# Cross-attention and LoRA-MoE kernel: product 7 taken jointly for two pairs, with the steps around it resequenced

## The chip, the core and the metric

The kernel runs on one core of one Trainium2 chip. The metric is device time in microseconds (us) for one execution. Engines: PE does matrix multiplications, DVE elementwise work, ACT activations and copies, POOL (GpSimd) elementwise work between SBUF tiles, and SP issues the DMAs.

## The reference, cut to what is computed

```python
# x (8,1024,1024), ctx (8,64,1024), mask (8,64), weight (1024,1024)
# lora_A (8,16,1024), lora_B (8,1024,16), router_w (8,1024); float32
h = layernorm(x)
scores = einsum('bsd,bmd->bsm', h, ctx) / 32
scores = where(mask, scores, -1e30)
x = x + einsum('bsm,bmd->bsd', softmax(scores), ctx)     # 0 where no mask is set
h = layernorm(x)
base   = einsum('btd,od->bto', h, weight)
logits = einsum('btd,ed->bte', h, router_w)
w_dense = top-2 of softmax(logits), renormalised, 0 elsewhere
Ax = einsum('nd,erd->ner', h, lora_A)
x = x + base + 2.0 * einsum('ner,ne,eor->no', Ax, w_dense, lora_B)
```

## The kernel before

The 8192 rows of x are 64 tiles of 128 rows. Two tiles are a *pair* u (32 pairs), held in SBUF as `xts[u][0]` and `xts[u][1]`; all work is float32. The function `first()` handles pairs 0 and 1 and prepares sums of the weights. After that `quad(u)`, u = 2, 4, ... 30, handles two pairs u and v = u+1 for the big product and, in the same stretch, prepares later pairs: n = u+2 and m = u+3 get their attention readout and second normalisation, and f = u+4 gets its scores and softmax. There are 15 such quads.

**The big product.** h times weight for a pair is a 2 by 2 block product taken in the Strassen-Winograd form: seven products instead of eight. `block_sums` forms on POOL the four sums of blocks of h that this needs (s1 to s4, each 128x512, four instructions), `weight_sums` formed the sums of weight blocks (t1 to t4) once. A product of 512 columns is a *block* of four matmuls (`block`, each recorded as two in the profile). `product(u, i)` runs product i = 1, 6 or 7 of one pair, all three into one PSUM bank `ch`, the running chain; after each, `product_add` adds the bank into one quarter of the pair's rows of x: 1 to (row tile 0, column half 0), 6 to (0, 1), 7 to (1, 0). `product(u, 8)` is the low-rank (LoRA) term for (1, 1), added to the same bank and then into x.

Products 5, 3, 2 and 4 are taken for the two pairs at once by `joint(i, u, hooks)`: here the pair of pairs is itself split 2 by 2, so that again seven blocks stand in place of eight, each of two matmuls of 256 columns. Its sums of activations come from `joint_sums` (POOL), its sums of weights from `quarter_sums` (DVE, four instructions on 128x512 a weight). A joint product writes two banks, `jl` (lower) and `ju` (upper), each holding two results of 256 columns. Blocks run in the order p4, chain, p2, p5, chain, p5, chain; between them DVE must read a result into x before the next block may write on top of it (`part`, `to_x`, the group at L716). Product 5 goes into both row tiles, so each of its reads is two DVE instructions. `hooks[k]` are steps recorded after the k-th block.

**Around it.** For each pair: `load_xs`/`load_xt` bring x twice, blocked (for turning) and plain; `att_turn` turns the blocked copy on DVE; `att_scores` (PE, 32 matmuls, L367), `att_sc` (one transpose on PE), `att_exp`, `att_divide`, `att_turn_p` (one transpose on PE), `att_readout` (PE, four matmuls, L420) and `att_add` (DVE, four adds) are the attention. `x_stats` is three ACT steps over the rows (`x_sums`, `x_squares`, `x_root`); `f_sums`, `f_squares`, `f_std`, `f_rows` do the second normalisation, of which `f_rows` begins with two small DVE instructions, writes h on ACT and sends it through DRAM (`norm_send`, `norm_fetch`) so that it comes back blocked; `rt_turn` turns it (four DVE instructions for a pair). `rt_low_rank_tile` (PE, L513) gives LoRA and router products of one row tile, the second one ends with a copy on ACT; `rt_top` is the routing on DVE (some 17 small instructions, with one exponential on ACT between them); `rt_turn_low_rank` (PE, two transposes, L553) needs its result. `mask_bias`, `send_mem`, `turn_mem`, `void_mem` prepare the context of a new batch; that is so in every second quad (u = 4, 8, ... 24).

**Order.** The whole schedule is manual: each engine runs its instructions in the order in which the code records them. A step that waits therefore holds up all that is recorded behind it on its engine. SP issues all DMAs in one such queue. Tiles with one tag share `bufs` buffers of a pool, and a new tile waits for the last reader of the buffer it gets; `ring` (6 buffers of 128x1024) holds xs, turned x, h, and h fetched back.

Of the kernel before, what the change touches and what calls it, by code (L numbers as in the profile page):

```python
# [17 lines left out]
P = 128  # L18
# [6 lines left out]
def kernel(  # L25
# [38 lines left out]
    ring = ctx.enter_context(tc.tile_pool(name="ring", bufs=6))  # L64
# [59 lines left out]
    def load_w(kh: int, oh: int):  # L124
# [10 lines left out]
    mask_u8 = const.tile([P, B, M], U8, name="mask_u8")  # L135
    nc.sync.dma_start(
        out=mask_u8.rearrange("p b m -> p (b m)"),
        in_=mask.rearrange("b m -> (b m)").partition_broadcast(P),
    )
# [24 lines left out]
    def mask_bias(b: int):  # L164

        biases[b] = memp.tile([P, M], F32, tag="bias", name=f"bias_{b}")
        nc.vector.tensor_copy(biases[b], mask_u8[:, b, :])
        valids[b] = memp.tile([P, 1], F32, tag="valid", name=f"valid_{b}")
        nc.vector.tensor_reduce(valids[b], biases[b], AX.X, ALU.max)
        nc.vector.tensor_scalar(biases[b], biases[b], NEG, -NEG, ALU.mult, ALU.add)  # L170
# [17 lines left out]
    def x_sums(u: int):  # L188

        sm = small.tile([P, 2, 1], F32, tag="sm", name=f"sm_{u}")  # L190
        nm = small.tile([P, 2, 1], F32, tag="nm", name=f"nm_{u}")
        for r in range(2):
            nc.scalar.activation(  # L193
                nowhere, xts[u][r], AF.Identity, accum_out=sm[:, r, :]
            )
        nc.scalar.mul(nm, sm, -1.0 / D)
        stds[u] = nm

    def x_squares(u: int):
        ss = small.tile([P, 2, 1], F32, tag="ss", name=f"ss_{u}")  # L200
        for r in range(2):
            nc.scalar.activation(  # L202
                nowhere, xts[u][r], AF.Square, bias=stds[u][:, r, :],
                accum_out=ss[:, r, :],
            )
        stds[u] = ss

    def x_root(u: int):

        ss = stds[u]  # L210
        stds[u] = small.tile([P, 2, 1], F32, tag="std_att", name=f"std_att{u}")
        nc.scalar.activation(stds[u], ss, AF.Sqrt, bias=eps_sb[:, 1:2])
# [13 lines left out]
    def x_std(u: int):  # L226
        mv = xmv.pop(u)
        stds[u] = small.tile([P, 2, 1], F32, tag="std_att", name=f"std_att{u}")
        nc.scalar.activation(
            stds[u], mv[:, :, 1:2], AF.Sqrt, bias=eps_sb[:, 1:2], scale=float(D)  # L230
        )

    junk = const.tile([P, D], mybir.dt.bfloat16, name="junk")
# [4 lines left out]
    def f_sums(u: int):  # L238

        sm = small.tile([P, 2, 1], F32, tag="smf", name=f"smf_{u}")  # L240
        nm = small.tile([P, 2, 1], F32, tag="nmf", name=f"nmf_{u}")
        for r in range(2):
            nc.scalar.activation(
                nowhere, xts[u][r], AF.Identity, accum_out=sm[:, r, :]
            )
        nc.scalar.mul(nm, sm, -1.0 / D)
        fts[u] = nm

    def f_squares(u: int):
        nm = fts[u]  # L250
        ss = small.tile([P, 2, 1], F32, tag="ssf", name=f"ssf_{u}")
# [4 lines left out]
        fts[u] = nm, ss  # L256

    def f_std(u: int):
        nm, ss = fts[u]
        std = small.tile([P, 2, 1], F32, tag="stdf", name=f"stdf_{u}")  # L260
        nc.scalar.activation(std, ss, AF.Sqrt, bias=eps_sb[:, 0:1], scale=1.0 / D)
        fts[u] = nm, std

    def f_rows(u: int, fetch: bool = True):

        nm, std = fts.pop(u)
        rstd = small.tile([P, 2, 1], F32, tag="rstdf", name=f"rstdf_{u}")
        nc.vector.reciprocal(rstd, std)
        nmr = small.tile([P, 2, 1], F32, tag="nmrf", name=f"nmrf_{u}")
# [104 lines left out]
    def att_rstd(u: int):  # L374
        sts[u] = small.tile([P, 2, 1], F32, tag="rstd_att", name=f"rstd_att{u}")
        nc.vector.reciprocal(sts[u], stds.pop(u))
# [6 lines left out]
    def att_exp(u: int):  # L383
# [6 lines left out]
        mx = small.tile([P, 2], F32, tag="mx", name=f"mx_{u}")  # L390
        nc.vector.tensor_reduce(mx, s, AX.X, ALU.max, negate=True)
        den = small.tile([P, 2], F32, tag="den", name=f"den_{u}")
# [5 lines left out]
        ps[u] = s, den  # L398

    def att_divide(u: int):  # L400
        s, den = ps[u]
        rden = small.tile([P, 2], F32, tag="rden", name=f"rden_{u}")
# [30 lines left out]
    def norm_stats(u: int, r: int, at_once: bool = True):  # L433
        mv = small.tile([P, 2], F32, tag=f"mv_ffn{r}", name=f"mv_ffn{u}_{r}")
        row_stats(mv, xts[u][r], f"ffn{u}_{r}")
# [4 lines left out]
    def norm_std(u: int, r: int):  # L440
        mv = nst[u, r]
        std = small.tile([P, 1], F32, tag=f"std_ffn{r}", name=f"std_ffn{u}_{r}")
# [3 lines left out]
    def norm_rows(u: int, r: int, here: bool):  # L446

        mv, std = nst.pop((u, r))
        rstd = small.tile([P, 1], F32, tag=f"rstd_ffn{r}", name=f"rstd_ffn{u}_{r}")
# [68 lines left out]
    def rt_top(u: int):  # L518
# [6 lines left out]
        dl = small.tile([P, 2, 1], F32, tag="dl", name=f"dl_{u}")  # L525
        tt(dl, top[:, :, 1:2], top[:, :, 0:1], ALU.subtract)
        e2 = small.tile([P, 2, 1], F32, tag="e2", name=f"e2_{u}")
# [3 lines left out]
        idf = small.tile([P, 2, 2], F32, tag="idf", name=f"idf_{u}")  # L531
# [5 lines left out]
        w1 = small.tile([P, 2, 1], F32, tag="w1", name=f"w1_{u}")  # L537
        nc.vector.tensor_scalar(w1, e2, 1.0, None, ALU.add)
        nc.vector.reciprocal(w1, w1)
        w2 = small.tile([P, 2, 1], F32, tag="w2", name=f"w2_{u}")  # L540
# [32 lines left out]
    def rt_sums_steps(u: int):  # L573
# [3 lines left out]
            sums.tile([P, 2, HK, P], F32, tag=f"s{i}", name=f"s{i}_{u}").rearrange(  # L577
                "p h k i -> p (h k) i"
            )
            for i in (2, 3)  # L580
# [7 lines left out]
    def rt_sums(u: int):  # L588
        for do in rt_sums_steps(u):
            do()  # L590
# [17 lines left out]
    def quarter_sums(name: str, w):  # L608
# [4 lines left out]
        tt(q3, b22, b12, ALU.subtract)  # L613
        tt(q2, q3, b11, ALU.add)
        tt(b12, b12, b11, ALU.subtract)
        tt(q4, b21, q2, ALU.subtract)
# [39 lines left out]
    def product_add(u: int, i: int):  # L656
# [4 lines left out]
        else:  # L661
            add(u, chain, *{1: (0, 0), 6: (0, 1), 7: (1, 0), 8: (1, 1)}[i])


    L2 = {2: (0, 0), 3: (0, 1), 4: (1, 0), 5: (None, 1)}
# [14 lines left out]
    def joint_sums(i: int, u: int):  # L680

        tags = "s2", "s3", "q3", "q4"
        outs = [
            sums.tile([P, 2, HK, P], F32, tag=t, name=f"{t}_j{i}_{u}") for t in tags
# [9 lines left out]
    def joint(i: int, u: int, hooks, final: bool = False):  # L694
# [6 lines left out]
        r, c = L2[i]  # L701
        a, d = [
            {2: hbs[p][:, 0], 3: sms[p][:, 1], 4: hbs[p][:, 1], 5: sms[p][:, 0]}[i]
# [3 lines left out]
        name = {2: "w21", 3: "w22", 4: "t4", 5: "t1"}[i]  # L707
# [4 lines left out]
        def to_x(p, src, first: int, n: int):  # L712
            cols = slice(c * HB + first, c * HB + first + n)
            for row in (0, 1) if r is None else (r,):
                xc = xts[p][row][:, cols]
# [65 lines left out]
    def add_and_stats(u: int, r: int):  # L781
# [5 lines left out]
        mv = small.tile([P, 2], F32, tag=f"mv_ffn{r}", name=f"mv_ffn{u}_{r}")  # L787
        nc.vector.bn_aggr(mv, st)
# [5 lines left out]
    def first():  # L794
# [70 lines left out]
        load_mem(1)  # L865
        att_divide(1)
# [37 lines left out]
        rt_sums(1)  # L904
# [57 lines left out]
        quarter_sums("t1", t1)  # L962
        att_scores(4)
# [11 lines left out]
    def quad(u: int):  # L975
# [7 lines left out]
        product(u, 1, (lambda: att_sc(n)) if u == 2 else None, 1)  # L983
        pending.pop()()
        product_add(u, 1)
        rt_low_rank_tile(u, 0)
        rt_turn(v)
        product(u, 6)
        if more:
            x_stats(m)  # L990
        if u == 2:
            att_divide(n)
            att_turn_p(n)
        if more:
            att_turn(m)
        product_add(u, 6)
        if u == 2:
            quarter_sums("t4", t4)
        if new_mem:
            mask_bias(b)  # L1000
            send_mem(b)
        if far:
            load_xs(f)
            load_xt(f)
        rt_low_rank_tile(u, 1)
        product(u, 7)
        rt_top(u)
        product_add(u, 7)
# [5 lines left out]

        if more:
            product(v, 1, {0: lambda: att_sc(m), 2: lambda: product(u, 8)})
            att_rstd(m)
            att_exp(m)
            one, two = rt_sums_steps(v)
            one()  # L1020
            product_add(u, 8)
            product_add(v, 1)
            two()
            f_sums(n)
            att_divide(m)
            rt_low_rank_tile(v, 0)
            product(v, 6, lambda: att_turn_p(m), 1)
            f_squares(n)
        else:
            rt_sums(v)  # L1030
            product(v, 1, {0: lambda: rt_turn_low_rank(u), 2: lambda: product(u, 8)})
            product_add(u, 8)
            product_add(v, 1)
            rt_low_rank_tile(v, 0)
            product(v, 6)
        if far:
            att_turn(f)
        product_add(v, 6)
        rt_low_rank_tile(v, 1)
        product(v, 7)  # L1040
        if new_mem:
            turn_mem(b)
        rt_top(v)
        if more:
            f_std(n)
            f_rows(n)
        product_add(v, 7)
        one, two = joint_sums(5, u)
        one()
        if more:  # L1050
# [3 lines left out]
        if u == 2:  # L1054
            quarter_sums("w21", w21)
# [3 lines left out]
        two()  # L1059

# [4 lines left out]
        if more:  # L1065
            hooks = {2: [low_v]}
# [4 lines left out]
        if far:  # L1071
            x_sums(f)
            x_squares(f)
            x_root(f)
            hooks[3] = [lambda: att_sc(f)]
        end_5 = joint(5, u, hooks)

        hooks = {1: [end_5]}
# [3 lines left out]
        if far:  # L1082
            hooks[2] = [lambda: att_rstd(f), lambda: att_exp(f)]
            hooks[7] = [lambda: att_divide(f)]
        end_3 = joint(3, u, hooks)
        if m + 2 < NP:
            load_xs(m + 2)
            if (f + 2) % PPB == 0 and f + 2 < NP:
                load_mem((f + 2) // PPB)

        one, two = joint_sums(2, u)
        one()
        hooks = {1: [end_3], 2: [two]}
        if more:
            f_squares(m)
            f_std(m)
            hooks[1].append(lambda: f_rows(m, False))
# [5 lines left out]
        def rows_0():  # L1103
# [5 lines left out]
            if more:  # L1109
                norm_fetch(m)  # L1110
# [4 lines left out]
        if more:  # L1115
            hooks[5] = [lambda: rt_sums(n)]
# [59 lines left out]
```

## Time and profile before

| what | value |
|---|---|
| median of 3 runs | 1124.63 us (1124.46 to 1125.69) |
| the profiled execution's own time | 1124.92 us |
| its span from first to last instruction | 1123.1 us |
| POOL busy in the span | 312.4 us (28%) |
| clock granted to PE | full in every slice |
| PE waiting for another engine, all named waits together | under 6 us, most of it before 21 us |
| quads 4, 6, 8, ... (start to start of the first product) | 68.2 us each |
| quad 2 | 69.15 us |
| x rows (512 KB), issue to landing | 6.5 us median |
| stores of x (512 KB), issue to landing | 3.5 us median |

A row of a timeline below gives start, length, engine, line, operation, output and inputs, shape and count. Lengths of matmuls include the tail of a pipeline, so the pace of PE is read from start to start. L613 to L616 are the four instructions of `quarter_sums`, L564 to L569 those of `block_sums`, L622 the adds of `add`.

### The profile page before, as it was taken

Reading aid. Unit: us, or ns where it says so; the run is one execution under the profiler, and the core shown is the slowest. Engines: PE = TensorE matmul, PEld = TensorE weight load, DVE = VectorE, ACT = ScalarE, POOL = GpSimd, SP = SyncE. Lnnn points to the kernel's source line nnn. Section 1 sums busy time; section 2 is a strip of 40 time slices with the busy share of each in tenths; the row PEclk is TensorE's granted clock in tenths of the full one; section 3 lists DMA queues with packets and bytes.
Section 4 is the critical chain, followed back from the end, with each engine's and each line's share of the span. In section 5 each row is a group of like instructions: output and inputs, shape, how many; then the busy total and the mean of one; then the engine's idle time right before and its main releaser. Section 6 shows DMA issues by size and latency. Waiting matters only on the chain.

```text
span 1123.1 us, 15874 instructions
## 1 busy us (share of the span) xinstructions
PE 1113.6 (99%) x5490; PEld 774.0 (69%) x5490; DVE 743.1 (66%) x1855; ACT 553.4 (49%) x1047; POOL 312.4 (28%) x260
## 2 busy tenths in 40 slices
PE   8999999999999999999999999999999999999998
PEld 6555576675867768676685866758677686766867
DVE  6679887666676566866568656686666766665544
ACT  4575562735537354472635736356373544725010
POOL 0022233142223323233132331432233232331331
PEclk9999999999999999999999999999999999999999
DMA  9966255562654726538363464535545454452401
GB/s 222 232 197 197 75 169 186 171 203 93 180 175 139 243 86 181 166 114 262 99 193 122 151 225 131 188 125 161 184 132 188 158 161 151 113 188 75 151 1 75
DMA packets 104464, 175.75 MB, mean 156 GB/s; under 512 B 11904, under 2 KB 76544, under 8 KB 104384
## 3 DMA queue, kind: packets, MB, share of 16 engines
q1 hardware_dynamic: 104384, 174.73, 50.6%
q8 instruction: 44, 0.72, 0.3%
q14 instruction: 36, 0.29, 0.1%
HBM read 107.84 MB, written 66.85 MB: 156 GB/s over the span
## 4 chain that ended last, share of the span: by engine, by line
PE 98%; DVE 1%; DMA 0%; ACT 0%; issue 0%; SPq 0%; DVEq 0%; ACTq 0%
PE ch L633 28%; PE jl L633 18%; PE ju L633 14%; PE pa L513 11%; PE ro L420 5%; PE sct L367 5%; PE ju L625 3%; PE jl L625 3%; PE plain L633 3%; PE ch L625 2%; PE trw L553 1%; PE j L633 1%; DMA xt<-in_x_dram 0%; PE ptp L409 0%; PE tr_x L342 0%; DVE xt L622 0%
## 5 line engine op out<-in xcount | busy, mean ns | idle before, releaser
L716 DVE TENSOR_TENSOR xt<-jl,xt 128x256 f32<-128x256 f32 (+1 forms) x301 | 140.0, 486 | 164.5 <-PE jl L633 111.2
L633 PE MATMUL ch<-t,s 128*128 128x512 f32 x496 | 224.7, 592 | 0.0
L193 ACT ACTIVATE junk<-xt 128x1024 bf16<-128x1024 f32 x60 | 63.3, 1055 | 206.3 <-DMA xt<-in_x_dram 205.3
L633 PEld LDWEIGHTS ch<-t,s 128*128 128x128 f32 x496 | 88.5, 190 | 86.2 <-issue 86.1
L622 DVE TENSOR_TENSOR xt<-ch,xt 128x512 f32<-128x512 f32 x124 | 85.0, 685 | 58.8 <-PE ch L633 34.6
L716 DVE TENSOR_TENSOR xt<-ju,xt 128x256 f32<-128x256 f32 (+1 forms) x150 | 80.3, 552 | 63.5 <-PE ju L633 62.6
L633 PE MATMUL ch<-w,hA 128*128 128x512 f32 x248 | 115.9, 593 | 0.0
L564 POOL TENSOR_TENSOR s<-hA,hB 128x512 f32<-128x512 f32 x31 | 39.6, 1278 | 266.0 <-DVE hB L89 201.6
L274 ACT ACTIVATE h<-xt,nmrf,rstdf 128x1024 f32<-128x1024 f32 x60 | 71.2, 1233 | 39.9 <-DVE nmrf L270 39.9
L622 DVE TENSOR_TENSOR xt<-ro,xt 128x512 f32<-128x512 f32 x128 | 81.3, 683 | 11.9 <-PE ro L420 11.9
L513 PEld LDWEIGHTS pa<-art_sb,hA 128*128 128x128 f32 x512 | 68.5, 190 | 23.2 <-issue 18.6
L89 DVE STREAM_TRANSPOSE xT<-xs 128x1024 f32<-128x1024 f32 x60 | 71.3, 1218 | 5.8 <-DMA xs<-in_x_dram 5.8
L633 PEld LDWEIGHTS ch<-w,hA 128*128 128x128 f32 x248 | 44.7, 190 | 43.0 <-issue 42.1
L564 POOL TENSOR_TENSOR s_j<-s 128x512 f32<-128x512 f32 x15 | 19.1, 1275 | 187.4 <-PE ch L633 187.4
L202 ACT ACTIVATE junk<-xt,nm 128x1024 bf16<-128x1024 f32 x60 | 68.9, 1149 | 2.0
L513 PE MATMUL pa<-art_sb,hA 128*128 128x136 f32 x512 | 69.9, 279 | 0.0
L513 PE MATMUL pa<-art_sb,hB 128*128 128x136 f32 x512 | 69.7, 279 | 0.0
L253 ACT ACTIVATE junk<-xt,nmf 128x1024 bf16<-128x1024 f32 x60 | 68.8, 1146 | 1.1
L367 PEld LDWEIGHTS sct<-xT,memT_True 128*64 128x64 f32 x960 | 51.8, 137 | 22.7 <-issue 17.4
L564 POOL TENSOR_TENSOR s_j<-hB 128x512 f32<-128x512 f32 x15 | 19.0, 1268 | 172.5 <-PE ju L633 172.5
L513 PEld LDWEIGHTS pa<-art_sb,hB 128*128 128x128 f32 x512 | 64.1, 190 | 0.0
L420 PE MATMUL ro<-mem,pt 64*128 64x512 f32 x256 | 63.6, 615 | 0.4 <-ACT pt L411 0.4
(183 smaller groups left out, 2090.0 us busy)
## 6 DMA issues: line engine op xcount, KB each, us to landing
xt<-in_x_dram SPq DMA_DIRECT2D x64, 512.0 KB, 6.5
out_dram<-xt SPq DMA_DIRECT2D x62, 512.0 KB, 3.5
xs<-in_x_dram SPq DMA_DIRECT2D x240, 128.0 KB, 3.8
hd<-h SPq DMA_DIRECT2D x60, 512.0 KB, 2.7
hs<-hd SPq DMA_DIRECT2D x240, 128.0 KB, 3.4
mem<-in_ctx_dram SPq DMA_DIRECT2D x16, 256.0 KB, 5.5
w<-in_w_t_dram SPq DMA_DIRECT2D x16, 256.0 KB, 10.2
md<-memc_False SPq DMA_DIRECT2D x7, 256.0 KB, 2.9
```

Of the source, the lines that this page charges most:

```text
L89: nc.vector.transpose(dst.rearrange("p k (t i) -> p t k i", i=NB), src.rearrange("p t (k i) -> p t k i", i=NB),)
L202: nc.scalar.activation(nowhere, xts[u][r], AF.Square, bias=stds[u][:, r, :], accum_out=ss[:, r, :],)
L253: nc.scalar.activation(nowhere, xts[u][r], AF.Square, bias=nm[:, r, :], accum_out=ss[:, r, :])
L274: nc.scalar.activation(h, xts[u][r], AF.Identity, bias=nmr[:, r, :], scale=rstd[:, r, :])
L367: mm(sct[r * M : (r + 1) * M, :], mt[:, k, :], x_ts[u][r][:, k, :], start=(k == 0), stop=(k == KD - 1),)
L420: mm(ro, pts[u][rows, :], m[rows, ts(c, HB)], start=True, stop=True)
L513: mm(pa[:, r, :], h, art_sb[:, k, :], start=(k == 0), stop=(k == KD - 1))
L564: by(s1, a21, a22, ALU.add)
L622: tt(xc, bank, xc, ALU.add)
L625: mm(bank, axwts[u][:, r, :], lb_sb[:, c0 : c0 + n], start=alone, stop=True, skip_group_check=True)
L633: mm(bank, a[:, k, :], w[:, k, :], start=(start and k == 0), stop=(k == n - 1), skip_group_check=True)
L716: tt(xc, src, xc, ALU.add)
```

## The change

Product 7 becomes a fifth joint product, run ahead of the other four, in the order 7, 3, 5, 2, 4 (before: 5, 3, 2, 4). Its activations are the sums s3 of the two pairs; both row halves of x in column half 0 and 1 of row tile 1 take its result, as `BOTH` says. The chain of a pair then holds products 1 and 6 when it is added to both (0, 1) and (1, 0) (`chain_add`). For the new product, `joint_sums(7, u)` adds four POOL instructions of 256 columns a quad, and `quarter_sums("t3", t3)` four DVE instructions in `first()`.

The rest moves: both low-rank tiles of a pair stand before its product 6; turning of x and statistics of pair m stand right after the first product of a quad; `x_stats(5)` and the weight sums of w21 and t4 move from quad 2 into `first()`, the latter two from DVE to POOL; the second normalisation of m stands behind product 3 and its rows are fetched back at once; the low-rank step of v moves from hook 2 of the first joint product to hook 4. The tiles s2, s3 and the joint sums share four places, whose roles rotate. The ring has 5 buffers. Masks are loaded batch by batch, small tiles are merged, and the unused output of the statistics is bytes.

```diff
-    ring = ctx.enter_context(tc.tile_pool(name="ring", bufs=6))
+    ring = ctx.enter_context(tc.tile_pool(name="ring", bufs=5))
...
-    junk = const.tile([P, D], mybir.dt.bfloat16, name="junk")
+    junk = const.tile([P, D], U8, name="junk")
...
+    places = ["qa", "qb", "qc", "qd"]
+
+    def in_place(i: int, name: str):
+        return sums.tile([P, 2, HK, P], F32, tag=places[i], name=name)
...
-    def quarter_sums(name: str, w):
+    def quarter_sums(name: str, w, by=tt):
...
+    def chain_add(u: int):
+
+        for to in ((0, 1), (1, 0)):
+            add(u, pps[u][1], *to)
+
+    L2 = {2: (0, 0), 3: (0, 1), 4: (1, 0)}
+    BOTH = {5: ((0, 1), (1, 1)), 7: ((1, 0), (1, 1))}
...
     def joint_sums(i: int, u: int):
+        if i == 7:
+            s12 = in_place(0, f"s12_j7_{u}")
+            s43 = in_place(2, f"s43_j7_{u}")
+            outs = jss[7] = s12[:, 0], s12[:, 1], s43[:, 1], s43[:, 0]
+            up, lo = [sss[p][2] for p in (u, u + 1)]
+            return block_sums(outs, up[:, :HK], up[:, HK:], lo[:, :HK], lo[:, HK:])
...
         quarter_sums("t1", t1)
+        quarter_sums("t3", t3)
+        x_stats(5)
+        for name, w in ("w21", w21), ("t4", t4):
+            quarter_sums(name, w, nc.gpsimd.tensor_tensor)
         att_scores(4)
...
         product(u, 1, (lambda: att_sc(n)) if u == 2 else None, 1)
+        if more and u > 2:
+            att_turn(m)
+            x_stats(m)
         pending.pop()()
         product_add(u, 1)
         rt_low_rank_tile(u, 0)
+        rt_low_rank_tile(u, 1)
         rt_turn(v)
-        product(u, 6)
-        if more:
-            x_stats(m)
         if u == 2:
             att_divide(n)
-            att_turn_p(n)
-        if more:
             att_turn(m)
-        product_add(u, 6)
-        if u == 2:
-            quarter_sums("t4", t4)
         if new_mem:
             mask_bias(b)
             send_mem(b)
+        product(u, 6, (lambda: att_turn_p(n)) if u == 2 else None, 1)
+        rt_top(u)
+        chain_add(u)
         if far:
             load_xs(f)
             load_xt(f)
-        rt_low_rank_tile(u, 1)
-        product(u, 7)
-        rt_top(u)
-        product_add(u, 7)
...
+        one, two = rt_sums_steps(v, (2, 3))
+        one()
+        two()
+        product(v, 1, low_u)
...
+        one, two = joint_sums(7, u)
+        one()
...
+        rt_low_rank_tile(v, 0)
+        rt_low_rank_tile(v, 1)
+        product(v, 6, (lambda: att_turn_p(m)) if more else None, 1)
+        two()
         if far:
             att_turn(f)
-        product_add(v, 6)
-        rt_low_rank_tile(v, 1)
-        product(v, 7)
...
         rt_top(v)
+        if more:
+            f_squares(n)
+        chain_add(v)
         if more:
             f_std(n)
             f_rows(n)
-        product_add(v, 7)
-        one, two = joint_sums(5, u)
-        one()
-        if more:
             att_readout(m)
...
-            hooks = {2: [low_v]}
+            hooks = {4: [low_v]}
...
-        end_5 = joint(5, u, hooks)
-
-        hooks = {1: [end_5]}
+        end_7 = joint(7, u, hooks)
+        one, two = joint_sums(5, u)
+        one()
+        two()
+
+        hooks = {1: [end_7]}
...
         end_3 = joint(3, u, hooks)
+
+        hooks = {1: [end_3]}
+        if more:
+            f_squares(m)
+            f_std(m)
+            hooks[1].append(lambda: f_rows(m))
+        end_5 = joint(5, u, hooks)
...
-        hooks = {1: [end_3], 2: [two]}
+        hooks = {1: [end_5], 2: [two]}
         if more:
-            f_squares(m)
-            f_std(m)
-            hooks[1].append(lambda: f_rows(m, False))
             hooks[5] = [lambda: rt_turn_tile(n, 1)]
```

## The prediction

> **What bounds the kernel now.** I read the page first. PE is busy for 99% of the span, and the chain of work that ended last lies on PE for 98% of it:
>
> ```profile
> PE   8999999999999999999999999999999999999998
> PE 98%; DVE 1%; DMA 0%; ACT 0%; issue 0%; SPq 0%; DVEq 0%; ACTq 0%
> ```
>
> So less PE work is time won, unless another engine makes PE wait. Next I read PE's timeline of one steady quad (start 515.55, the next starts at 583.77):
>
> ```profile
> 521.27 3.60 PE L633 MATMUL ch<-t,s 128*128 128x512 f32 x8
> 524.71 1.09 PE L513 MATMUL pa<-art_sb,hA 128*128 128x136 f32 x8
> ...
> 557.01 1.03 PE L633 MATMUL ju<-w,s_j 128*128 128x256 f32 x4
> 557.88 1.03 PE L633 MATMUL jl<-t,s_j 128*128 128x256 f32 x4
> 558.98 1.10 PE L633 MATMUL ju<-w,q_j 128*128 128x256 f32 x4
> 559.92 1.03 PE L633 MATMUL jl<-t,q_j 128*128 128x256 f32 x4
> 560.78 1.03 PE L633 MATMUL jl<-w,s 128*128 128x256 f32 x4
> ```
>
> From start to start a 512-column block takes 524.71 - 521.27 = 3.44, a 256-column block 0.86. The third row starts at 557.01 and the fourth 0.87 later, but the fifth 1.10 after the fourth: product 5 is read into two row tiles, and DVE is not through with it:
>
> ```profile
> 558.08 0.76 DVE L716 TENSOR_TENSOR xt<-ju,xt 128x256 f32<-128x256 f32 x2 [1.15 <-PE ju L633]
> ```
>
> A double read is done 0.97 after PE's block (557.87 to 558.84), and PE goes on 0.14 later: 1.11 against a cover of 0.86, so 0.25 is lost there; another 0.08 at 559.92.
>
> Last I read where `first()` runs into quad 2, in the timelines of DVE, POOL and PE:
>
> ```profile
> 98.84 1.39 DVE L613 TENSOR_TENSOR w<-w 128x512 f32<-128x512 f32 x1
> 100.27 1.64 DVE L614 TENSOR_TENSOR w<-w,w 128x512 f32<-128x512 f32 x1
> 101.83 1.75 DVE L615 TENSOR_TENSOR w<-w 128x512 f32<-128x512 f32 x1
> 103.51 1.76 DVE L616 TENSOR_TENSOR w<-w,w 128x512 f32<-128x512 f32 x1
> ...
> 105.79 0.68 DVE L613 TENSOR_TENSOR t<-w 128x512 f32<-128x512 f32 x1
> ...
> 109.89 0.68 DVE L622 TENSOR_TENSOR xt<-ch,xt 128x512 f32<-128x512 f32 x1
> ```
>
> ```profile
> 98.42 1.26 POOL L564 TENSOR_TENSOR s<-hA,hB 128x512 f32<-128x512 f32 x1 [34.89 <-DVE hB L89]
> 99.77 1.59 POOL L565 TENSOR_TENSOR s<-s,hA 128x512 f32<-128x512 f32 x1
> ```
>
> ```profile
> 110.91 3.60 PE L633 MATMUL ch<-t,s 128*128 128x512 f32 x8
> 114.34 0.27 PE L409 MATMUL ptp<-ident,s 128*128 128x128 f32 x1
> ```
>
> While POOL adds, the same DVE instruction takes 1.39 to 1.76 in place of 0.68, and the two take turns, one of each in some 1.6. DVE instructions that read PSUM, and turnings, keep their length beside POOL. The add at 109.89 frees the chain for product 6 at 110.91: 0.34 of room.
>
> **The change part by part.** The baseline is this execution: span 1123.1, 1.8 around it, 1124.92 in all, 0.29 over the median of 1124.63. Differences are applied to the median.
>
> (a) Product 7. Each quad loses two 512-blocks, 2 x 3.44 = 6.88, and gains seven 256-blocks, 7 x 0.862 = 6.03. That is -0.85 a quad, on PE, 15 times: **-12.8**.
>
> (b) Reads of the new product. It too is read twice. Between its first p5 block and the one that overwrites it lies the low-rank step of v (0.86 of cover more), so that one is free. But the add of that step (0.69) stands on DVE before the second double read: chain block ends, 0.21 to DVE, 0.76, 0.14 back, 1.11 against 0.86: 0.25 lost. Product 5 loses its low-rank neighbour and keeps 0.25 of its 0.33. Net +0.17 a quad: **+2.6**. Bounds 0 to 0.4 a quad, 0 to +6.
>
> (c) `first()` into quad 2. DVE's queue gets t3's four instructions before the last adds of pair 1, the softmax of pair 4 and the add of product 1 (pair 2), which product 6 waits for. POOL gets eight sums (w21, t4) right behind its four of 98.42 to 104.72, so DVE's four of t1 (0.63 apart before) and four of t3 all run beside POOL. Eight by 1.6 from 105.8 is 118.6; the last meets an idle POOL, say 118.1. In the trace 2.25 lie between the end of the sums (108.32) and the end of that add (110.57), so 120.4, and 0.15 to PE: 120.5. PE, now with both low-rank tiles first (109.06 + 2 x 1.85), is there at 112.76: it stands for 7.7. Then the transpose of pair 4's softmax comes two matmuls into product 6, at 122.2, but DVE has first to turn four tiles and divide, 2.77 behind the add in the trace: 123.2 with the way back, another 1.0. The routing of pair 2, beside POOL's sums for pair 3, is late by some 0.5. Against that, quad 2 took 69.15, 0.93 over its followers (windows of the quads), because the sums of w21 ran late on DVE; this goes. Together 7.7 + 1.0 + 0.5 - 0.9 = **+8.3**. If POOL did not matter, t3 alone would be four by 0.63 = 2.5 later: 110.57 + 2.5 + 0.15 - 112.76 = 0.5, and 1.0 + 0.5 - 0.9 as above: +1.1. If each pair took 1.75, the longest row, +9.5. I take the upper part, as the rows that show both engines are those of the same instructions a few us earlier.
>
> A rule speaks against moving sums to POOL. The Trainium skill, "SBUF — State Buffer", section "Who interferes with whom", says that a DVE instruction with two SBUF inputs and a GpSimd one that reads SBUF lock each other out for the whole instruction. By that each turn costs the unblocked lengths together, 1.27 + 0.63 = 1.9, and (c) would be 2.4 more; the rows show 1.6, which I use.
>
> (d) Steady quads: is everything in time with less cover? I laid the new order on the trace's lengths, from a quad's start. PE reaches the routing transposes of u at 15.1 (18.35 before: one 512-block of 3.44 less stands ahead of them). Routing starts when the LoRA copy is out of ACT, which runs the statistics of m first; these wait for x of m. Before, its loads were issued behind eight fetches and landed 6.2 into the quad, and routing ended at 16.1 (531.6). Now the fetches are ahead of the stores, the loads follow the stores' landing (3.5) at about 1.5 before the quad's end, with 3 to 4 to land: x is there at about 2, ACT is free by 8, routing ends at 12 to 13. Cost nothing; covered by 2. If the landing is as late as before, routing ends at 15.4 to 16.1: 0.5 to 1.2 a quad.
>
> In quads with new context, 3.77 of DVE work (457.84 to 461.61) now stands between the turning of v (ends 7.8) and the routing, which takes 3.3: 14.9 to 15.7, so 0.2 to 0.9 late; I take 0.5. There the scaling of the context (1.15 on ACT, after attention's copies) also pushes the second normalisation of m, whose two small DVE instructions stand ahead of the reads of product 5: in other quads they end about 0.5 ahead of need (statistics of f from 33, softmax 42.9, root 47.7, reads done 48.9, needed 49.4), here 0 to 0.9 late; I take 0.4. Six quads by 0.9: **+5.4**; bounds 0 and 6 x 1.8 = 10.8.
>
> (e) At nothing. POOL's sums: the last of rt_sums(v) ends at about 13 and is needed at 23; those of product 3 are ready 5 to 8 ahead, those of product 2 three. The four extra POOL instructions are 256 wide, about 0.65 each, in idle time (POOL 28%). DVE gets some 6.7 a quad more on 43 to 47 of 68, which shows only where (b) to (d) say. Ring of 5: xs of the next m waits for a turned tile used 25 earlier; xs of pair 4 in `first()` is issued some 10 later (behind a turning at 66) and used at 91; h of pair 3 starts 0.6 later, and is fetched by 106, used at 120. SP: the stores of pair 1 wait for (c), which holds xs of pair 6 until 127; used at 136. Masks, merged small tiles, byte output: ACT's 1.06 and 1.15 for such rows hardly differ from its 1.23 with float output; bounds -0.1 and +0.1 each, off the path but for (d).
>
> Sum: -12.8 + 2.6 + 8.3 + 5.4 = +3.5: 1128.1.
>
> **Rivals.** *Gain stands* (faster). DVE's order into quad 2 costs only the uncontended +1.1, and new-context quads have room: -12.8 + 2.6 + 1.1 + 0 = -9.1: 1115.5; with half of (c), 1119. For it: 0.25 to 0.9 in (d) is small against what I can lay out by hand. Against it: the rows at 98.84. *Only (c) bites* (no change): -12.8 + 2.6 + 8.3 = -1.9: 1122.7. *Late x* (slower): x of m lands as late as before, and PE waits at the routing transposes. In the seven other quads that have an m that costs the 0.5 to 1.2 of (d), 3.5 to 8.4; in the six with new context routing stands behind that DVE work anyway, and some 0.5 more each is 3. Together 6.5 to 11.4 on top of my sum, the middle 9: 1137; decided at a landing beyond 4 into the quad. For it: median landing 6.5 on the page; against it: nothing else is in flight then.
>
> **How the numbers follow.** Forecast 0.40 (own range 1125 to 1132), gain stands 0.26, only (c) 0.20, late x 0.14; together 1. Within 0.2% means within 2.2 of 1124.6, about what this kernel's measurement can tell from no change. Faster: gain stands, less a little, plus a third of only (c): 0.30. Slower: late x, and the forecast with what part of it falls short: 0.53. Same: 0.17. The range goes to 1115 at the fast end and 1134 at the slow one.
>
> **What would show it.** (a): quads whose PE blocks sum to 0.85 less. (b): a gap of 0.25 before the new product's last block. (c): PE idle for 7 to 9 before product 6 of quad 2, and L613 to L616 instructions of 1.4 to 1.8 up to 118. (d): PE waiting at `trw` for DVE in quads 4, 8, 12 and not in 6, 10; the first ACT row of each quad at about 2. Steady quads of 67.5, and 68.4 with new context. I am wrong if quad 2 is not longer than before, or if every quad waits.

## The result, and the profile after

The changed kernel takes 1138.52 us (median of 4 runs, 1138.36 to 1139.44) against 1125.16 for the kernel before on the same chip: a ratio of 1.0119 (95% interval 1.0102 to 1.0137). It is slower by more than was forecast, and outside the range. The profiled execution has a span of 1136.7, 13.6 more than before.

On the page of the changed kernel, PE's row of the slices, the clock granted to PE in the same slices (in tenths of full speed, 9 is full), and the chain of work that ended last:

```profile
PE   8999799999999999999999999999999999999998
PEclk9999899999999999999999999999999999999999
PE 84%; DVE 10%; ACT 2%; DMA 2%; issue 1%; SPq 0%; DVEq 0%; ACTq 0%
```

A tenth of the chain has gone from PE to DVE, and in the fifth slice (113.7 to 142.1) the clock is not full, as it was everywhere before. The list of PE's waits (engine, line, waited for, total, times, longest) says where:

```profile
PE trw L551 <- DVE axl L545: 11.0, 9, 1.5
PE ch L635 <- DVE xt L624: 8.1, 1, 8.1
```

The 8.1 is one wait ahead of product 6 of quad 2, term (c) of the prediction. The 11.0 is the routing (`trw` is its transpose on PE), the other place. From the start of the first product of each quad to that of the next (quad 30: to the last matmul), by PE's timelines:

| stretch | before | after | later runs: both mended | and halves, t1 on POOL |
|---|---|---|---|---|
| up to quad 2 | 105.41 | 104.80 | 104.99 | 105.18 |
| quad 2 | 69.06 | 78.42 | 70.07 | 68.82 |
| quads 4, 8, ... 24 (new context), each | 68.22 | 69.22 | 67.65 | 67.33 |
| quads 6, 10, ... 26, each | 68.22 | 67.65 (10 and 14: 67.87) | 67.65 | 67.33 |
| quad 28 | 66.10 | 65.86 | 65.85 | 65.61 |
| quad 30 | 59.41 | 61.40 | 58.86 | 58.86 |

After less before, added up: -0.61 + 9.36 + 6 x 1.00 - 3.0 - 0.24 + 1.99 = 13.5, the whole difference. (The stretch up to quad 2 differs by up to 1.7 between profiled executions, whatever the edit; the quads repeat within 0.02 where no wait is in them. Quad 2 of the kernel before is 69.06 from start to start, not the 69.15 of the first table.)

**Quad 2.** DVE's, POOL's and PE's timelines where `first()` runs into it:

```profile
105.19 1.15 DVE L615 TENSOR_TENSOR t<-w 128x512 f32<-128x512 f32 x1
106.38 1.64 DVE L616 TENSOR_TENSOR t<-t,w 128x512 f32<-128x512 f32 x1
...
116.31 1.74 DVE L618 TENSOR_TENSOR t<-t,t 128x512 f32<-128x512 f32 x1
117.98 0.68 DVE L624 TENSOR_TENSOR xt<-j,xt 128x512 f32<-128x512 f32 x1
...
119.55 0.68 DVE L624 TENSOR_TENSOR xt<-ch,xt 128x512 f32<-128x512 f32 x1
```

```profile
104.08 1.72 POOL L615 TENSOR_TENSOR w<-w 128x512 f32<-128x512 f32 x1
...
115.81 1.71 POOL L618 TENSOR_TENSOR t<-t,t 128x512 f32<-128x512 f32 x1
```

```profile
120.38 3.75 PE L635 MATMUL ch<-t,s 128*128 128x512 f32 x4 [8.07 <-DVE xt L624]
123.92 0.42 PE L409 MATMUL ptp<-ident,s 128*128 128x128 f32 x1
```

DVE's eight sums of t1 and t3 go from 105.19 to 117.98, 1.60 each, with POOL's eight sums of w21 and t4 beside them, one by one. The add that product 6 waits for is at 119.55.

The wait is not the whole cost. By the profile's windows the clock granted to PE is 0.50 from 115.35 to 125.59: it falls 3.0 after PE stopped and is full again 5.2 after PE went on. In the rows above, the two matmuls of 120.38 take 3.54 from start to start, where two such matmuls take 1.72 at full clock. Quad 2 is 10.77 longer than the 67.65 of an undisturbed quad; 8.07 is the wait, no other wait of PE in it is over 0.1, and the 2.70 that is left fits 5.2 at half clock, which is 2.6 lost.

**Quad 30** has no other pair's work in it, so it shows the routing alone. DVE before, DVE after, POOL before, POOL after (part of each):

```profile
1071.58 0.17 DVE L532 CAST idf<-idx 128x4 f32<-128x4 uint32 x1
1071.79 0.26 DVE L536 TENSOR_TENSOR we<-iota_e,idf 128x16 f32<-128x16 f32 x2
...
1072.71 0.16 DVE L541 TENSOR_TENSOR w<-w,e 128x2 f32<-128x2 f32 x1
...
1073.32 0.49 DVE L547 TENSOR_TENSOR axl<-axl,we 128x128 f32<-128x128 f32 x2
```

```profile
1080.16 1.03 DVE L532 CAST of_top<-idx 128x4 f32<-128x4 uint32 x1
1081.23 1.33 DVE L536 TENSOR_TENSOR we<-iota_e,of_top 128x16 f32<-128x16 f32 x2
...
1082.67 0.17 DVE L538 RECIPROCAL of_top<-of_top 128x2 f32<-128x2 f32 x1
1082.88 0.91 DVE L539 TENSOR_TENSOR of_top<-of_top 128x2 f32<-128x2 f32 x1
...
1084.64 1.02 DVE L545 TENSOR_TENSOR axl<-axl,we 128x128 f32<-128x128 f32 x2
```

```profile
1073.85 1.27 POOL L569 TENSOR_TENSOR s<-hA 128x512 f32<-128x512 f32 x1 [2.60 <-PE ch L633]
```

```profile
1079.90 1.26 POOL L563 TENSOR_TENSOR s<-s,hA 128x512 f32<-128x512 f32 x1
1081.25 1.28 POOL L566 TENSOR_TENSOR s<-hB,s 128x512 f32<-128x512 f32 x1
1082.50 1.27 POOL L567 TENSOR_TENSOR s<-hA 128x512 f32<-128x512 f32 x1
```

Before, POOL's last sum waited for PE and came when the routing was over; the routing took 3.0 (1070.79 to 1073.81). After, it takes 6.7 (1078.92 to 1085.59): the cast of 1080.16 lasts until POOL's sum of 1079.90 is over at 1081.16, the instructions of 1081.23 until the sum of 1081.25 is over at 1082.53, and so on. Reciprocals, MAX8 and the search for an index keep their length. PE, ready at 1083.45 (1081.73 + two matmuls of 0.86), begins each transpose late:

```profile
1081.73 1.88 PE L635 MATMUL ch<-w,hA 128*128 128x512 f32 x4
1085.08 0.30 PE L551 MATMUL trw<-ident,axl 128*128 128x128 f32 x1 [1.47 <-DVE axl L545]
1085.72 0.33 PE L551 MATMUL trw<-ident,axl 128*128 128x128 f32 x1 [0.34 <-DVE axl L545]
```

**Quad 4, with new context.** On DVE, the preparation of the context meets the same POOL instructions:

```profile
191.34 1.04 DVE L172 TENSOR_SCALAR bias<-bias 128x64 f32<-128x64 f32 x1
...
193.91 1.65 DVE L296 TENSOR_SCALAR memc_False<-mem,mv_mem 64x1024 f32<-64x1024 f32 x1
195.48 0.22 DVE L524 MAX8 top<-axl 128x8 f32<-128x8 f32 x2
...
199.28 0.49 DVE L545 TENSOR_TENSOR axl<-axl,we 128x128 f32<-128x128 f32 x2
```

The preparation takes 4.6 where I had 3.8, the routing 4.2 where I had 3.3, and PE waits 1.51.

### The profile page after: what moved, and what is told of

Read it like the earlier page. It is cut to its first block, busy times and chain, and to the rows that moved or that the text cites. A ratio compares the mean times of both kernels' runs of the same rounds, so it can differ in the third digit from the quotient of the medians.

```text
span 1136.7 us, 16623 instructions
## 1 busy us (share of the span) xinstructions
PE 1108.7 (98%) x5670; PEld 806.3 (71%) x5670; DVE 845.3 (74%) x2031; ACT 548.2 (48%) x1045; POOL 371.3 (33%) x328
## 4 chain that ended last, share of the span: by engine, by line
PE 84%; DVE 10%; ACT 2%; DMA 2%; issue 1%; SPq 0%; DVEq 0%; ACTq 0%
PE jl L635 23%; PE ju L635 17%; PE ch L635 15%; PE pa L513 8%; PE sct L366 4%; PE ro L420 4%; PE jl L627 3%; PE ju L627 3%; PE plain L635 2%; PE ch L627 2%; DMA xt<-in_x_dram 1%; PE trw L551 1%; DVE memc_False L296 1%; DMA out_dram<-xt 1%; DVE we L536 1%
## 5 line engine op out<-in xcount | busy, mean ns | idle before, releaser
L732 DVE TENSOR_TENSOR xt<-jl,xt 128x256 f32<-128x256 f32 (+1 forms) x421 | 191.8, 485 | 132.1 <-PE jl L635 111.8
L195 ACT ACTIVATE junk<-xt 128x1024 uint8<-128x1024 f32 x60 | 63.4, 1056 | 193.4 <-DMA xt<-in_x_dram 192.8
L635 PE MATMUL ch<-t,s 128*128 128x512 f32 x256 | 119.5, 603 | 8.1 <-DVE xt L624 8.1
L635 PE MATMUL jl<-t,s_j 128*128 128x256 f32 x360 | 93.5, 382 | 1.1
L635 PE MATMUL ju<-w,s_j 128*128 128x256 f32 x360 | 94.0, 383 | 0.0
L273 ACT ACTIVATE h<-xt,of_f 128x1024 f32<-128x1024 f32 x60 | 71.3, 1234 | 21.6 <-DVE of_f L269 20.6
L635 PEld LDWEIGHTS jl<-t,s_j 128*128 128x128 f32 x360 | 65.9, 190 | 22.2 <-issue 12.7
L635 PEld LDWEIGHTS ju<-w,s_j 128*128 128x128 f32 x360 | 64.1, 190 | 16.6 <-DVE xt L732 5.8
L204 ACT ACTIVATE junk<-xt,of_x 128x1024 uint8<-128x1024 f32 x60 | 68.9, 1149 | 1.9
L253 ACT ACTIVATE junk<-xt,of_f 128x1024 uint8<-128x1024 f32 x60 | 68.5, 1142 | 1.1
```

The source lines that it names most:

```text
L195: nc.scalar.activation(nowhere, xts[u][r], AF.Identity, accum_out=sm[:, r, :])
L204: nc.scalar.activation(nowhere, xts[u][r], AF.Square, bias=nm[:, r, :], accum_out=ss[:, r, :],)
L253: nc.scalar.activation(nowhere, xts[u][r], AF.Square, bias=nm[:, r, :], accum_out=ss[:, r, :])
L273: nc.scalar.activation(h, xts[u][r], AF.Identity, bias=nmr[:, r, :], scale=rstd[:, r, :])
L635: mm(bank, a[:, k, :], w[:, k, :], start=(start and k == 0), stop=(k == n - 1), skip_group_check=True)
L732: tt(xc, src, xc, ALU.add)
```

## The experiments

Two theories stood from here. *Turns*: DVE and POOL instructions that read SBUF hold each other up, in quad 2 and in every routing of u, which now runs at the time of POOL's sums of v. Its rivals put the waits down to DVE having more to do, or to work being put ahead.

### The quarter sums: t3 later; or w21 and t4 away from POOL

```diff
-        quarter_sums("t3", t3)              # in first()
...
             att_add(n)
+        if u == 2:
+            quarter_sums("t3", t3)
```

> The four quarter sums of t3 move from first() to quad 2, behind the readout's adds; nothing else. Theory 'turns' (DVE and POOL instructions that both read SBUF take turns of about 1.67 us a pair): four turns leave DVE's queue ahead of the add of product 1, so the 8.07 us for which PE stands before product 6 of quad 2 shrink by 4 x 1.67 = 6.7 to about 1.4; total 1138.5 - 6.7 = 1131.8. Rival 'length' (DVE's queue is too long even by unhindered lengths of 0.63): the wait shrinks by 2.5 only; total 1136.

Measured: 1132.53 (ratio to before 1.0065, 1.0048 to 1.0081), 6.0 less than the changed kernel. PE's list of waits in this run:

```profile
PE ch L635 <- DVE xt L624: 1.4, 1, 1.4
```

The 1.4 of *turns*, not the 5.6 of *length*. POOL beside it still has all its sums. The clock stays full in this quad 2, so the half clock of the changed kernel belongs to its long wait; and two waits show that PE did not have there while it was slow: 0.95 at the softmax of pair 4 and 1.20 at the routing of u.

```diff
-        for name, w in ("w21", w21), ("t4", t4):
-            quarter_sums(name, w, nc.gpsimd.tensor_tensor)
...
         chain_add(u)
+        if u == 2:
+            quarter_sums("t4", t4)
...
+        if u == 2:
+            quarter_sums("w21", w21)
         end_7 = joint(7, u, hooks)
```

> The quarter sums of w21 and t4 go back from POOL in first() to DVE in quad 2, where the kernel before had them; t1 and t3 stay where they are. Theory 'turns': POOL is silent after its four activation sums (about 104), so DVE's eight sums of t1 and t3 take 0.63 each, the add of product 1 ends near 112.5 and PE waits 0.5 in place of 8.07; less some 0.9 that these sums cost quad 2 on DVE, total about 1131.8. Rival 'length': DVE still has the same eight sums ahead of the add, the wait stays near 8; total 1138 to 1139.

Measured: 1134.02 (1.0080, 1.0063 to 1.0096). The eight sums of t1 and t3, as many as before and in the same place, run in 5.05 (106.68 to 111.73) in place of 12.8, and the wait is 0.4: *length* is out. The clock is full in quad 2 of this run too. But only 4.5 came back, where an end of the wait by itself would have given 7.6. The sums of w21 on DVE now stand ahead of the reads of product 7, for which PE waits 2.15 in quad 2, and once PE no longer comes late, it meets the softmax of pair 4 (0.8) and the routing of u (1.2) there: the 0.9 that was allowed for w21 and t4 on DVE was too small. This execution also lost 1.7 at 91, ahead of all that was edited (quad 2 starts at 106.22).

### What holds up the routing: turning behind it, context behind it

```diff
         rt_low_rank_tile(u, 1)
-        rt_turn(v)
...
         rt_top(u)
+        rt_turn(v)
         chain_add(u)
```

> In every quad the turning of h of pair v (DVE) moves from ahead of the routing of u to behind it; POOL's sums of v, which need it, start behind the routing too. Theory 'turns': the routing of u, 6.7 us long beside POOL's sums in plain quads and in quad 30, is 3.0 to 3.3 long again, PE's 11.0 us of waits for it go, also the 2 us in quad 30, where nothing else on DVE changes ahead of the routing; total about 1127. Rival 'work ahead' (the routing is late because DVE has the new context's 3.8 us to do first): in quads with new context the wait goes because 2.5 us of turning leave the way, but the routing's own length stays and quad 30 keeps its wait of 2; total about 1129.5.

Measured: 1129.02 (1.0034, 1.0023 to 1.0045), 9.5 less than the changed kernel. In quad 30, DVE and POOL of this run:

```profile
1071.58 0.17 DVE L532 CAST of_top<-idx 128x4 f32<-128x4 uint32 x1
...
1073.36 0.49 DVE L545 TENSOR_TENSOR axl<-axl,we 128x128 f32<-128x128 f32 x2
```

```profile
1076.33 1.27 POOL L562 TENSOR_TENSOR s<-hA,hB 128x512 f32<-128x512 f32 x1 [12.57 <-DVE hB L89]
```

POOL starts after the routing, which is 2.9 long again, and the cast 0.17. The preparation of the context shrinks too (0.75 for the centring). No wait for the routing is left in PE's list. The 2 that stayed of the expected 11.5 are in quads 4, 16 and 24, which are 0.3 to 0.9 longer than 67.65, and in quad 30, where PE waits 0.7 for the turned rows of v.

```diff
-        if new_mem:
-            mask_bias(b)
-            send_mem(b)
         product(u, 6, (lambda: att_turn_p(n)) if u == 2 else None, 1)
         rt_top(u)
         chain_add(u)
+        if new_mem:
+            mask_bias(b)
+            send_mem(b)
```

> In quads with new context the preparation of the context (mask bias, statistics, centring) on DVE moves behind the routing of u and the adds of product 6. Theory 'turns': the routing then runs beside POOL's sums as it does in plain quads, 8.2 to 14.9 after the quad's start, so 6 waits of 1.5 shrink to 0 to 0.2 each and the wait of 2 in quad 30 stays; total 1129.5 to 1131. Rival 'work ahead': the same in those quads, but then the routing there is 3.3 long, not 6.7.

Measured: 1175.75 (1.0454, 1.0437 to 1.0472): both theories were wrong by 45. Quads with new context take 74.2 to 75.3. The routing of quad 4 is 4.1 long (194.81 to 198.91) and PE waits 0.57 for it in place of 1.51, so in that much the move did what both said. But `send_mem` also issues DMAs, and these stand ahead of others. SP's queue in quad 4, the changed kernel first:

```profile
195.59 0.47 SPq L321 DMA_DIRECT2D md<-memc_False  x1
...
200.25 4.37 SPq L83 DMA_DIRECT2D xs<-in_x_dram  x8
```

```profile
203.00 0.47 SPq L321 DMA_DIRECT2D md<-memc_False  x1
...
207.70 3.74 SPq L83 DMA_DIRECT2D xs<-in_x_dram  x8
```

The centred context is ready 7.4 later, SP waits for it, and the loads of xs of pair f wait behind it on SP. DVE then stands for them, with the routing of v and all else in its queue:

```profile
212.17 1.25 DVE L89 STREAM_TRANSPOSE xT<-xs 128x1024 f32<-128x1024 f32 x1 [2.20 <-DMA xs<-in_x_dram]
```

A few instructions moved back by one place on DVE cost 5 to 6 in each of these quads. In four of the six the clock is also at half for 3.4, at most 1.7 of it; the other two are as long without it. That the path is the DMA queue, which the edit did not name, is read from these rows; no run moved the DMA issues alone.

### Both collisions taken away

```diff
-        quarter_sums("t1", t1)              # in first()
-        quarter_sums("t3", t3)
...
             att_divide(m)
+        if u == 2:
+            quarter_sums("t3", t3)
+            quarter_sums("t1", t1)
...
-        rt_turn(v)
+        rt_turn_tile(v, 0)
...
         rt_top(u)
+        rt_turn_tile(v, 1)
         chain_add(u)
```

> The changed kernel with both collisions taken away: t1's and t3's quarter sums move from first() to quad 2 behind att_divide(m); in every quad only row tile 0 of pair v is turned ahead of the routing of u, row tile 1 (which POOL's first sum needs) behind it. Theory 'turns': of the changed kernel's 1138.5, the 9.5 go that the run with the turning behind the routing saved, and in quad 2 the waits of 8.07 and 0.9; total 1119 to 1121. Rival 'the cost only moves': eight sums of 0.63 on DVE in quad 2, some beside POOL, delay the routing of v or the reads of product 7 there by 2 to 3 as the run with POOL free did with w21; total 1122 to 1124.

Measured: 1118.19 (0.9948, 0.9931 to 0.9965): faster than the kernel before. All steady quads take 67.65, with new context or without, and quad 30 has 58.86. In quad 2 two waits of 1.2 and 0.8 are left, so the rival had a small share. This is the change with its two collisions out: 67.65 - 68.22 = -0.57 a quad is what it brings by itself.

### The double reads of products 7 and 5

A block that is read twice needs 1.11 and is covered by 0.86. First I put another block between, in the kernel mended and in the kernel before:

```diff
+        if i in BOTH:                       # before: if i == 5
+            block(chain, a[:, :HK], b11, True)
+            part(u, 0, chain)
+            block(p5, s1, q1, True)
+            part(v, 1, p5)
+            block(p2, a[:, HK:], b21, True)
+            block(chain, s2, q2, False)
+            part(u, 1, chain)
+            block(p5, s4, b22, False)
+            block(p4, d[:, HK:], q4, True)
+            block(chain, s3, q3, False)
...
```

> As the run with both collisions taken away, and in joint products 7 and 5 the blocks run in the order chain, p5, p2, chain, p5, p4, chain, so that one block more lies between each block that DVE reads twice and the block that overwrites it. Theory 'double reads' (PE stands 0.25 + 0.08 in each of these products because two DVE instructions of 0.38 and the way there and back take 1.11 against a cover of 0.86): two gaps of 0.3 a quad go, 15 x 0.57 = 8.5 less than that run, about 1111. Rival: the gaps come from the bank or the sums on POOL and stay; the same time as that run.

Measured: 1165.67 (1.0362, 1.0344 to 1.0379).

> The kernel before with that order of blocks in joint product 5 alone, and nothing else. Theory 'double reads': its gaps of 0.25 + 0.08 a quad go, 15 x 0.33 = 5.0; total 1120. Rival: they stay; 1125.

Measured: 1141.82 (1.0154, 1.0137 to 1.0171). In these two runs products 7 and 5 (5 alone in the second) lose the part of a sum that was in a bank when p2 or p4 started in its other half. The same without the start mark on p2 and p4:

> The run with both collisions taken away (1118.2), and in joint products 7 and 5 the order of blocks chain, p5, p2, chain, p5, p4, chain; p2 and p4, which come second into a bank whose other half is still being summed, go without the start mark, which in the earlier attempt made PE wait 0.8 for DVE's reads of the whole bank. Theory 'double reads': the gaps of 0.25 + 0.08 in each of the two products go (cover 1.72 against 1.11), 15 x 0.57 = 8.5; total 1109.7. Rival: the gaps come from the bank, not from the reads; 1118.

Measured: 1166.43 (1.0366, 1.0349 to 1.0384).

> The kernel before with that order, and the start mark left off p2 and p4, in joint product 5 alone. Theory 'double reads': 15 x 0.33 = 5.0 less, 1120. Rival: 1125.

Measured: 1141.91 (1.0149, 1.0132 to 1.0166). All four are slower, by 17 to 48, than the kernel that each starts from, mark or no mark. PE in product 7 of quad 4, in the third of them:

```profile
213.56 1.03 PE L635 MATMUL ju<-t,s_j 128*128 128x256 f32 x4
...
215.54 1.13 PE L635 MATMUL ju<-t,s 128*128 128x256 f32 x4 [0.83 <-DVE xt L732]
```

The second row is p2, which writes the half of bank `ju` that nobody reads; it waits all the same for DVE's reading of p5 in the other half, and in product 5 for 1.55. So in this program a block waits for a read of its bank, whichever half is read; the runs show the wait, not what it is there for. A cover must be a block of another bank. These runs said nothing for or against *double reads*: my order had put a block of the same bank right behind each read.

> As the first of these, and the quarter sums of t3 and t1 in quad 2 on POOL, in its idle time of some 13 us between the first two and the last two sums for product 7. Theory 'turns': DVE is rid of 5.0 us there, the routing of v then runs beside POOL (3.1 becomes up to 6.7) but has 9 us; the waits of 1.2 and 0.8 that quad 2 has left in the mended run go, 2 less than the first of these. Rival: routing of v comes late by turns; 1 to 3 more than the first of these.

```diff
+        if u == 2:
+            for name, w in ("t3", t3), ("t1", t1):
+                quarter_sums(name, w, nc.gpsimd.tensor_tensor)
...
-        if u == 2:
-            quarter_sums("t3", t3)
-            quarter_sums("t1", t1)
```

Measured: 1165.48, 1 less than the same order without it, but not for the reason expected: quad 2 itself is 1.1 longer (76.56 after 75.46), as the rival said, and the profiled execution without it loses 1.7 in quad 28 to 3.4 at half clock, which the other does not have there. DVE is rid of 5 us, but the routing of v takes 8.1 beside these sums (129.23 to 137.34) and PE waits 1.2 for it: the collision once more, in a third place.

A step that is in another bank is the low-rank step of v. Cut in two, it covers both reads of product 7:

```diff
+        def low_v_half(k: int):
+            lora(v, pps[v][1][:, k * HH : (k + 1) * HH], 1, HB + k * HH, HH)
+            if k:
+                product_add(v, 8)
...
-            hooks = {4: [low_v]}
+            hooks = {4: [lambda: low_v_half(0)], 6: [lambda: low_v_half(1)]}
```

> The run with both collisions taken away (1118.2, steady quads of 67.65), and the low-rank step of pair v, which stands whole (0.86) ahead of the fifth block of joint product 7, split into two halves of 0.43: one ahead of the fifth block, one ahead of the seventh, the add behind the second; no block changes its bank or place. Theory 'double reads' (1.11 against 0.86): each of the two reads of product 7 is covered by 1.29, the gaps of 0.24 + 0.08 go, quads of 67.3; total 1118.2 - 15 x 0.33 = 1113.3. Rival 'the bank': the gaps stay; 67.65 and 1118.

Measured: 1113.99 (0.9909, 0.9892 to 0.9925); quads of 67.33. The last blocks of product 7 and the first of product 3 in the mended run, and then with the halves:

```profile
277.30 1.02 PE L627 MATMUL ch<-lb_sb,axwt 128*128 128x512 f32 x2
278.16 1.03 PE L635 MATMUL jl<-t,s_j 128*128 128x256 f32 x4
279.03 1.03 PE L635 MATMUL ju<-t,s_j 128*128 128x256 f32 x4
280.13 1.10 PE L635 MATMUL jl<-t,s_j 128*128 128x256 f32 x4
281.07 1.03 PE L635 MATMUL jl<-w,s 128*128 128x256 f32 x4
```

```profile
276.77 0.59 PE L627 MATMUL ch<-lb_sb,axwt 128*128 128x256 f32 x2
277.20 1.03 PE L635 MATMUL jl<-t,s_j 128*128 128x256 f32 x4
278.07 1.03 PE L635 MATMUL ju<-t,s_j 128*128 128x256 f32 x4
278.93 0.59 PE L627 MATMUL ch<-lb_sb,axwt 128*128 128x256 f32 x2
279.36 1.03 PE L635 MATMUL jl<-t,s_j 128*128 128x256 f32 x4
280.23 1.03 PE L635 MATMUL jl<-w,s 128*128 128x256 f32 x4
```

Start to start, 1.10 and 0.94 become 0.86 and 0.87: the gaps were the double reads. Those of product 5 (0.15 and 0.10) are still there; no step of another bank was at hand for them.

```diff
-            quarter_sums("t1", t1)         # behind t3, on DVE
...
         two()
+        if u == 2:
+            quarter_sums("t1", t1, nc.gpsimd.tensor_tensor)
```

> As the run with the halves, and t1's quarter sums in quad 2 on POOL behind its last sums for product 7, where POOL is idle for 4.4 us and the routing of v is over; DVE is rid of 2.5 us there. Theory 'turns': no overlap with instructions of DVE that read SBUF twice, the wait of 1.2 in quad 2 goes and quad 2 is 1 to 2 shorter than in the run with the halves. Rival: the routing of v meets these sums (as it met t3 and t1 together) and quad 2 is no shorter.

Measured: 1112.85 (0.9900, 0.9883 to 0.9916), quad 2 shorter by 0.94 (69.76 to 68.82). The wait of 1.2 is 0.3. The first of these sums (133.63) does meet the last step of the routing of v, which takes 1.51 in place of 0.49, but PE has no wait for it. This is the fastest version: 1.0% below the kernel before, 25.7 us below the changed one.

## Why the prediction was wrong

The forecast had the side right (slower, for DVE and POOL in each other's way) and the size wrong: +3.5 against +13.5 in the profiled executions. By its terms, measured against the 67.65 of an undisturbed quad:

| term | predicted | measured |
|---|---|---|
| (a) and (b), 15 quads | -10.2 | 15 x -0.57 = -8.6 |
| (c) `first()` into quad 2 | +8.3 | -0.61 + 9.36 + 0.57 = +9.3 |
| (d) six quads with new context | +5.4 | 6 x 1.57 = +9.4 |
| quads 10, 14 | 0 | +0.4 |
| quad 28 | 0 | +0.3 |
| quad 30 | 0 | 1.99 + 0.57 = +2.6 |

**(a), (b).** The step was right, the second gap mis-sized: product 7 shows 0.24 and 0.08 where I had one gap of 0.25, product 5 keeps the 0.25 that I gave it. The halves confirm the cause by 0.32 a quad.

**(c)** had its main step right: turns of 1.60 (1.6 forecast) and a wait of 8.07 (7.7). Taking the upper part of the bounds was right, for the reason given. But that the sum came within 1.0 is in part luck. The 1.0 at the softmax of pair 4 and the 0.5 of the routing do not show as waits in the changed kernel; in their place stands half clock behind the long wait, 2.7, which the prediction put at nothing. Without the long wait both small waits are there (0.95 and 1.20 in the run with t3 late). By the rule of the Trainium skill, "SBUF — State Buffer", section "Who interferes with whom", as the prediction applied it, a turn would have been an estimated 1.9; the run has 1.60 in the mean.

**(d) is the step that failed**, at the words that the routing "takes 3.3". That length was read where only one of POOL's sums of v (462.02) ran beside it, and it held the price of that one already, as the 3.77 of the context held another. DVE before, in that quad:

```profile
458.42 1.06 DVE L170 TENSOR_SCALAR bias<-bias 128x64 f32<-128x64 f32 x1
...
462.35 0.96 DVE L532 CAST idf<-idx 128x4 f32<-128x4 uint32 x1
```

Both are small, and with no sum of POOL beside them they take 0.19 and 0.17, as with the turning behind the routing. In the kernel before, the second and fourth sums waited for products 6 and 7 of u, and the routing began 11.6 into quad 30. In the changed kernel both low-rank tiles stand ahead of product 6, so it begins 8.2 into quad 30, and the sums of v find their places free and run from 7.8 to 13, as (e) of the prediction itself had said. I priced the turns where whole sums met on DVE and POOL, and not where POOL's sums met 17 small instructions, though the two stretches stood beside each other in my own working. The price was 3.7 in quad 30, 0.9 on the routing and 0.8 on the preparation in quads with new context. In plain quads the routing is 6.7 long as well, and ends just as PE arrives: the "covered by 2" was used up, which costs quads 10 and 14 the 0.2 that they show. The 0.4 that (d) gave to the reads of product 5 in quads with new context did not come: those quads have 1.57, of which 1.51 is the routing. Nor does its 0.2 to 0.9 for the routing follow from its own figures: 14.9 to 15.7 against 15.1 is 0.6 at most, or 0.75 with the 0.15 to PE.

**The rivals.** *Gain stands*, 1115.5 by its sum, was wrong for the kernel as changed; only with the collisions taken out is its gain there, 1118.2 and 0.57 a quad. *Only (c) bites* fell with (d). *Late x* did not decide: in plain quads ACT starts on x of m 1.0 into the quad and has the routing's row ready at 8.2; in quad 4 it starts at 2.9 and is ready at 10.4, but DVE comes to the routing at 12.3. With the turning behind the routing, the landing does set its start there (11.2 into quad 4), at almost no cost.

**(e)** held except for that: masks, merged tiles, byte output and the smaller ring show in no wait of PE's list. No run takes them out one by one.

## What to carry to other kernels

A step that is moved earlier, or a buffer that becomes free earlier, can bring two engines together that had hardly met before: lay their stretches on one line, and take a length only from a stretch with the same neighbours. A chain of small instructions pays the most, as each can wait for the rest of a long one. A long wait of PE can cost more than itself: 8.07 here brought 2.7 of half clock behind it, waits of up to 1.4 in the same place none. An edit on one engine is an edit on the DMA queue that its steps issue to, and here a cover for a read in PSUM had to be a block of another bank.

## What had not been expected of the hardware

It is not only DVE instructions with two inputs in SBUF that wait for POOL: in quad 30 a cast of 128x4 went from 0.17 to 1.03, and in quads with new context the centring of 64x1024 (one tensor input and a scalar for each partition) from 0.75 to 1.65. The mask's 128x64 takes 0.19 without POOL and 1.04 beside it; it took 1.06 in the kernel before already, as the cast took 0.96 in its quads with new context. The Trainium skill, "SBUF — State Buffer", section "Who interferes with whom", says that casts and `tensor_scalar` can contend with GpSimd when their operands allow a mode that uses both ports; the runs agree, and I had looked only at its sentence on two inputs. An operation on 128x2 values pays nearly as much (0.16 to 0.91) as one on 128x512 (0.63 to 1.6). POOL's own sums keep their 1.27 beside the small DVE instructions of quad 30 and stretch to 1.72 beside long ones. PE's clock at half, for 10.24 around a wait of 8.07, was not expected either: the run with the turning behind the routing has it too (10.24 around 8.04), those with a wait of 1.4 or less in this place do not. Shorter waits can bring it too, though not always: with t3 late, 3.4 at half follow waits of 1.8 in quad 30, where the changed kernel has waits as long and full clock.
